# A different first tile, Toeplitz blocks read straight from the taps, and a reordered opening in an attention-and-experts kernel

## The chip, the cores and the metric

The kernel runs on one core of one Trainium2 chip. The metric is the device time of one execution in microseconds (us): the median of three runs, 709.8 us (708.9 to 709.98).

## What is computed

Two layers follow each other. The first is a long convolution that stands in for attention: for each of 32 heads of width 8, all products of the rows of a head of `ctx_2048` (called k; it serves as k and v) are convolved along the 512 positions with the head's filter, a skip term is added, and the result is contracted with the layer-normed `x` (q). The second is a mixture of 16 experts with top-4 routing and a capacity of 256 tokens, plus a shared expert. Everything is float32.

```python
kv = einsum('bhil,bhjl->bijhl', k_, v_)                # k_ = v_ = ctx in heads of 8
y = irfft(rfft(kv, 1024) * rfft(ssm_kernel, 1024))[..., :512]
out = y + kv * D                                       # skip, one number per head
out = einsum('bijhl,bhil->bjhl', out, q_)              # q_ = layernorm(x) in heads
x = x + out
...
h = layernorm(x)
scores = softmax(h @ gate_w.T); top 4 of 16 experts, capacity 256
x = x + sum over chosen experts(silu(h Wg) * (h Wu)) Wd * weight
      + (silu(h sWg) * (h sWu)) sWd                    # shared expert, 704 wide
```

## The kernel before, in words

The 2048 rows (8 batches by 256) are cut into 16 tiles of 128 rows. A tile holds 16 rows of every batch, which is two heads of the convolution (`HT` = 2). The causal convolution is done on TensorE as products with 128x128 Toeplitz blocks: the tile `toep` of a head holds four blocks side by side (offsets 0, 128, 256, 384). A head is done in two halves (`attend`, line 390, called with `c0` = 0 and `c0` = 2, two output chunks of 128 positions each): the first half takes 3 matmuls (1 + 2), the second 7 (3 + 4), all 128x288 (`convolve`, line 404). The trace has two records for each such float32 matmul. From head `PLAIN` = 6 on (tile 3 on) the second half uses five prepared blocks, of which one product, `shared`, serves both chunks: 6 matmuls, a copy of `shared` on ScalarE (line 422) and an extra addition on VectorE (line 427).

The Toeplitz blocks come out of DRAM by overlapping reads, one position further per partition. For the first six heads `blocks` (line 358) reads them from `pad_d`, a copy of the filters with 128 zeros ahead of each and the skip number added to the first tap (lines 257 to 263: two loads on ScalarE's queue, an addition on VectorE at line 262, and the store, on ScalarE's queue again). For the others it reads `win_d`, which `windows` (line 264) writes from `pad` and from two differences, `less` (line 269, GpSimd). A head's `toep` has one of 4 buffers, and `y` in PSUM one of 2.

The steps of a tile, by engine:
- SP's queue loads `kn` (k) and `xs` (x) of a tile (`load_tile`, line 308: k first, then x), 256 KB each.
- TensorE transposes k and normalised q (line 126, four 128x128 transposes each); ScalarE copies the result into `k2`/`q2` (lines 354, 355) and normalises (lines 305, 306). The first two tiles take mean and variance on VectorE (`first_statistics`, line 290: 296, 297, 298) and the root on GpSimd (299, 300); later ones on ScalarE (280 to 285) and GpSimd (286, 287). Tiles from 3 on get k and q into heads by way of DRAM (`send_blocks`, `fetch_blocks`: `sent`, `got`).
- GpSimd forms the products `kv` (`products`, line 374): one of 128x128 (line 379), then four of 128x256 (line 381), chunk by chunk, and from `PLAIN` on a sum of two chunks (line 387).
- VectorE multiplies `y` with q and adds (lines 437, 442, 448, 453, 454). Two smaller sums follow (456, 457): on VectorE for heads below `PLAIN`, on GpSimd for the others.
- `add_to_x` transposes the tile's output back (line 465) and adds it to x (line 467); `new_statistics`, `normalise` and line 646 make the normed, transposed `xnT` of the tile for the second layer; `by_feature` (line 485) computes router logits (line 489) and picks the top experts.

The order is written out by hand: each engine runs its instructions in the order in which the program gives them. The loop over tiles (line 575) does `attend` of tile n and prepares tile n+1 and finishes tile n-1 in between. The shared expert's work (`shared_block`, line 129) is cut into pieces by `yield`; `fill(count)` slips pieces between the halves from the time a tile is ready (`ready`, line 566), so TensorE has work from tile 2 on. Its weights (`swg`, `swu`, `swt`, `swd`) are loaded in 17 pieces by `load_shared(9)`, nine per tile, on SP's queue (line 529). The first product of the first block (line 141, `sgt`) needs both halves of `swt`, which are pieces 9 and 10: the second half is the first piece of tile 1's share. Then come the experts, one after the other (lines 901 on).

All loads named stand in SP's one queue in program order; a wait there holds what is behind it.

Of the kernel before, what the change touches and what calls it, by code (L numbers as in the profile page):

```python
# [20 lines left out]
P = 128  # L21
# [3 lines left out]
NC = L // P  # L25
# [11 lines left out]

ND = HD // 2
PAIRS = ND * HB + HB // 2
PLAIN = 3 * 2  # L40
KW = HB + 3 * B
QW = HB + 4 * B
BACK = 2 * B
# [9 lines left out]
def ssm_attention__then__moe_kernel(  # L53
# [64 lines left out]
    def by_tile(rows):  # L118

        return rows.rearrange("(b n r) l -> n r b l", b=B, n=NT)  # L120
# [126 lines left out]
    with ExitStack() as att:  # L247
# [6 lines left out]

        pad = half.tile([S // HD, P + L], F32, name="pad", tag="k2")
        dcol = const.tile([S // HD, 1], F32, name="dcol")
        nc.vector.memset(pad[:, 0:P], 0.0)
        nc.scalar.dma_start(out=pad[:, P:], in_=ssm)  # L260
        nc.scalar.dma_start(out=dcol, in_=skip)
        nc.vector.tensor_add(pad[:, P : P + 1], pad[:, P : P + 1], dcol)
        nc.scalar.dma_start(out=pad_d[:, :], in_=pad)
        def windows():


# [40 lines left out]

        def load_tile(n):
            kn = load.tile([P, L], F32, name="kn")
            nc.sync.dma_start(out=kn, in_=by_tile(ctx_in)[n])  # L310
            nc.sync.dma_start(out=xs[:, n, :], in_=by_tile(x)[n])
            return kn

        def in_blocks(name):
# [34 lines left out]
        def heads_of(src, width, name):  # L349


            dst = half.tile([P, NC, HT, width], F32, name=name)
            pt = transpose_in(src).rearrange("p c (h w) -> p c h w", h=HT)
            nc.scalar.copy(dst[:, :, :, 0:HB], pt)
            nc.scalar.copy(dst[:, :, :, HB:width], pt[:, :, :, 0 : width - HB])
            return dst
# [33 lines left out]
        def attend(head, hh, c0, toep, kv, q2, oT):  # L390
# [61 lines left out]
            )  # L452
            nc.vector.tensor_mul(yd, yd, view(qq, 0, [[qc, 2], [B, ND], [1, HB]]))  # L453
            nc.vector.tensor_add(f, yd, z[:, :, :, BACK : BACK + HB])  # L454
            adder = nc.vector if head < PLAIN else nc.gpsimd
            adder.tensor_add(f[:, :, 0:2, :], f[:, :, 0:2, :], f[:, :, 2:4, :])  # L456
            adder.tensor_add(
                oT[:, c0 : c0 + 2, hh * HB : (hh + 1) * HB], f[:, :, 0, :], f[:, :, 1, :]
# [23 lines left out]
        def store(n, xn):  # L482
            nc.sync.dma_start(out=by_tile(xw_d[0:T, 0:L])[n], in_=xn)

        def by_feature(n):

            lg = ps_tr.tile([P, E], F32, name="lg", tag="pt")
            for c in range(NC):
                nc.tensor.matmul(  # L489
                    lg, lhsT=xnT[:, c, n, :], rhs=gwT[:, c, :], start=(c == 0), stop=(c == NC - 1)  # L490
                )
            nc.vector.tensor_copy(logits[:, n, :], lg)

            top = tops[:, n, :]
            nc.vector.max(out=top, in_=logits[:, n, :])
            nc.vector.memset(tops[:, n, K:8], 3.0e38)
            rest = small.tile([P, E], F32, name="rest")
            nc.vector.match_replace(
                out=rest, in_to_replace=top, in_values=logits[:, n, :], imm_value=-3.0e38
            )  # L500
            nc.vector.tensor_tensor(sel[:, n, :], rest, logits[:, n, :], ALU.is_lt)

            if n == 0:
                nc.vector.memset(early[:, 0, :], 0.0)
            nc.gpsimd.tensor_add(early[:, n + 1, :], early[:, n, :], sel[:, n, :])

        toeps = {}

        def load_blocks(head):
            toeps[head] = blocks(head)  # L510
# [17 lines left out]
                dst, src = shared_pieces.pop(0)  # L528
                nc.sync.dma_start(out=dst, in_=src)

        loaded = {0: load_tile(0)}
        gw = load.tile([E, L], F32, name="gw", tag="kn")
        nc.sync.dma_start(out=gw, in_=gate_w)
        loaded[1] = load_tile(1)
        load_blocks(0)
        load_blocks(1)

        qn = load.tile([P, L], F32, name="qn", tag="kn")
        k2 = heads_of(loaded.pop(0), KW, "k2")
        stats = first_statistics(xs[:, 0, :])  # L540
        kvs = [products(0, 0, k2)]
        normalise(qn, xs[:, 0, :], *stats)
        kvs.append(products(1, 1, k2))
        q2 = heads_of(qn, QW, "q2")
        pg = ps_tr.tile([P, NC, P], F32, name="pg", tag="pt")
        for c in range(NC):
            nc.tensor.transpose(pg[:, c, 0:E], gw[:, c * P : (c + 1) * P], ident[:E, :E])
        nc.scalar.copy(gwT, pg[:, :, 0:E])

        blocks_left = [(t, 1) for t in range(4)] + [(t, 2) for t in range(4, NT, 2)]
        behind = []

        def fill(count):
# [9 lines left out]

        def ready(n):

            by_feature(n)
            if n + 1 == sum(blocks_left[0]):
                behind.append(shared_block(*blocks_left.pop(0)))  # L570

        making = masks()
        oT_done = None
        sent_k = sent_q = sent_x = got_x = None
        for n in range(NT):
            more = n + 1 < NT
            swift = n + 1 in SWIFT
            oT = work.tile([P, NC, P], F32, name="oT")
            tps = [toeps.pop(n * HT + hh) for hh in range(HT)]
            if more:  # L580
                for hh in range(HT):
                    load_blocks((n + 1) * HT + hh)
            for t in range(2 if n == 0 else n + 3, min(n + 4, NT)):
                loaded[t] = load_tile(t)
            if swift and more:
                got_k, got_q = fetch_blocks(sent_k), fetch_blocks(sent_q)
            load_shared(9)
            if n == 1:
                windows()
            if n:  # L590
                attend(n * HT + 0, 0, 0, tps[0], kvs[0], q2, oT)
            if n - 2 in MILD:
                transpose_blocks(xnT[:, :, n - 2, :], got_x)
            if more:
                if not swift:
                    qn = load.tile([P, L], F32, name="qn", tag="kn")
                    stats = (
                        statistics(qn, xs[:, n + 1, :]) if n else first_statistics(xs[:, 1, :])
                    )
            if n == 0:  # L600
                attend(n * HT + 0, 0, 0, tps[0], kvs[0], q2, oT)
            fill(2)
            if n + 2 in SWIFT:
                kp, kp_by_block = in_blocks("kp")
                kp_stats = statistics(kp_by_block, chunked(xs[:, n + 2, :]))

            attend(n * HT + 0, 0, 2, tps[0], kvs[0], q2, oT)
            if more and not swift:
                k_next = heads_of(loaded.pop(n + 1), KW, "k2")
                normalise(qn, xs[:, n + 1, :], *stats)  # L610
            if n > 0:
                total = add_to_x(n - 1, oT_done)
            fill(2)
            if n > 0:
                xn, xstats = new_statistics(n - 1, total)
            if more:
                if swift:
                    k_next = heads_from(got_k, KW, "k2")
                kv_next = [products((n + 1) * HT, 0, k_next)]

            attend(n * HT + 1, 1, 0, tps[1], kvs[1], q2, oT)
            if more and not swift:
                q_next = heads_of(qn, QW, "q2")
            fill(2)
            if n > 0:
                normalise(xn, xs[:, n - 1, :], *xstats)
                store(n - 1, xn)
                if n - 1 in MILD:
                    xp, by_block = in_blocks("xp")
                    normalise(by_block, chunked(xs[:, n - 1, :]), *xstats)  # L630
                    sent_x = send_blocks(xp)
            if more:
                if swift:
                    q_next = heads_from(got_q, QW, "q2")
                kv_next.append(products((n + 1) * HT + 1, 1, k_next))
            if n + 2 in SWIFT:
                nc.scalar.copy(kp_by_block, chunked(loaded.pop(n + 2)))
                sent_k = send_blocks(kp)
            if n - 2 in MILD:
                ready(n - 2)  # L640

            attend(n * HT + 1, 1, 2, tps[1], kvs[1], q2, oT)
            if n - 1 in MILD:
                got_x = fetch_blocks(sent_x)
            elif n > 0:
                nc.scalar.copy(xnT[:, :, n - 1, :], transpose_in(xn))
                fill(1)
                ready(n - 1)
            fill(1)
            if n + 2 in SWIFT:  # L650
                qp, by_block = in_blocks("qp")
                normalise(by_block, chunked(xs[:, n + 2, :]), *kp_stats)
                sent_q = send_blocks(qp)
            if n in (6, 7, 8):
                next(making)
            oT_done = oT
            if more:
                kvs, q2 = kv_next, q_next
# [5 lines left out]
        nc.scalar.copy(xnT[:, :, NT - 1, :], transpose_in(xn))  # L664
        fill(1)
        by_feature(NT - 1)
        store(NT - 1, xn)
        behind.extend(shared_block(*b) for b in blocks_left)
        fill(1)
# [296 lines left out]
```

## Time and profile before

| what | value |
|---|---|
| time, median of 3 runs | 709.8 us |
| the profiled execution's own time | 708.86 us |
| its span, first to last instruction | 707.1 us |
| TensorE (PE) busy | 679.8 us, 96% |
| VectorE (DVE) busy | 371.4 us, 53% |
| GpSimd (POOL) busy | 294.1 us, 42% |
| ScalarE (ACT) busy | 195.3 us, 28% |
| mean granted TensorE clock | 0.988 |

So 1.8 us of the execution's time lie outside the span, and its time is 0.9 us below the median. A row of the timeline gives the start in us from the span's start, the duration of the stretch, the engine (SPq and ACTq are queues that issue transfers), the line, the operation, what is written <- what is read, and how many records; in brackets stands the idle time before it and what ended it. A row of the windows gives, for a stretch, its length, then busy time and number of records of each engine, the granted TensorE clock, the share of time that the DMA engines were busy, and GB/s. A chain row is one step of the path that ended last.

### The profile page before, as it was taken

The numbers are of one execution on the slowest core, as the hardware profiler recorded it, in microseconds if no ns is written. First come the engines' busy times: TensorE is split into PE (matmuls) and PEld (weight loads), VectorE is DVE, ScalarE is ACT, GpSimd is POOL, SyncE is SP. The second block draws the span as 40 slices with busy tenths as digits, with TensorE's granted clock in tenths as the row PEclk, the third lists the DMA queues.
The fourth block names the chain that finished last, engine by engine and source line by source line (L and its number), as shares of the span: only waits on it lengthen the run. The fifth ranks groups of instructions, "written<-read, shape, count | busy, mean of one in ns | idle before, by whom it ended". The sixth has DMA issues, their size and how long they took to land.

```text
span 707.1 us, 9801 instructions
## 1 busy us (share of the span) xinstructions
PE 679.8 (96%) x3419; PEld 512.1 (72%) x3419; DVE 371.4 (53%) x858; ACT 195.3 (28%) x498; POOL 294.1 (42%) x455
## 2 busy tenths in 40 slices
PE   5899999899999999999999999999999999999994
PEld 3677977777877876876867685777777777777772
DVE  2977666768877676766536411333343334433221
ACT  2443333443432443322222011221222111121120
POOL 5544446767656776556210200233223333322221
PEclk9999999999999999999999999999999999999998
DMA  7942454746566456451019211577777677777732
GB/s 201 308 121 53 128 156 110 184 129 162 148 156 182 115 123 170 127 142 44 16 31 315 58 46 31 168 186 200 217 200 210 186 197 195 209 194 202 190 45 30
DMA packets 89616, 104.03 MB, mean 147 GB/s; under 512 B 10256, under 2 KB 61808, under 8 KB 89568
## 3 DMA queue, kind: packets, MB, share of 16 engines
q1 hardware_dynamic: 82256, 86.22, 43.0%
q0 software_dynamic: 7168, 17.04, 11.7%
q8 instruction: 27, 0.44, 0.3%
q10 hardware_dynamic: 144, 0.15, 0.1%
q14 instruction: 21, 0.17, 0.1%
HBM read 75.73 MB, written 27.66 MB: 146 GB/s over the span
## 4 chain that ended last, share of the span: by engine, by line
PE 90%; DVE 4%; DMA 3%; issue 1%; ACT 1%; SPq 0%; POOLq 0%; POOL 0%; ACTq 0%; DVEq 0%
PE sgu L155 20%; PE y L404 16%; PE pgu L842 15%; PE eo L884 12%; PE so L172 11%; PE pgu L862 4%; PE pt L126 2%; PE pgu L854 2%; PE shared L404 2%; PE sgt L141 2%; PE lg L489 2%; PE ip L747 1%; DMA got<-sent 1%; DVE y L453 1%; PE pt L465 1%; DVE f L454 1%
## 5 line engine op out<-in xcount | busy, mean ns | idle before, releaser
L404 PE MATMUL y<-kv,toep 128*128 128x288 f32 x536 | 145.8, 418 | 3.6 <-POOL rstd L286 2.1
L404 PEld LDWEIGHTS y<-kv,toep 128*128 128x128 f32 x536 | 104.1, 197 | 36.6 <-issue 5.0
L842 PE MATMUL pgu<-xgT,w 128*128 128x256 f32 (+1 forms) x544 | 113.8, 367 | 0.8 <-ACT xgT L814 0.8
L842 PEld LDWEIGHTS pgu<-xgT,w 128*128 128x128 f32 x544 | 98.6, 190 | 20.4 <-issue 7.7
L893 POOL DMA_INDIRECT out<-eo_sb,idx x32 | 51.0, 1595 | 105.6 <-DMA out<-eo_sb,idx 49.3
L801 POOL DMA_INDIRECT g<-xw_d,idx x32 | 32.0, 999 | 141.7 <-PE eo L884 62.4
L381 POOL TENSOR_TENSOR kv<-k 128x256 f32<-128x256 f32 x128 | 86.6, 707 | 0.0
L884 PE MATMUL eo<-wd,mid 128*128 128x512 f32 (+1 forms) x192 | 86.4, 598 | 0.0
L155 PE MATMUL sgu<-xnT,swg 128*128 128x256 f32 (+1 forms) x400 | 78.1, 338 | 1.8 <-DVE tail L149 1.8
L155 PE MATMUL sgu<-xnT,swu 128*128 128x256 f32 (+1 forms) x400 | 78.5, 340 | 0.0
L456 POOL TENSOR_TENSOR f<-f 128x256 f32<-128x256 f32 x52 | 37.9, 728 | 94.6 <-DVE f L454 89.5
L172 PE MATMUL so<-swd,smid 128*128 128x512 f32 x160 | 74.4, 594 | 0.0
L155 PEld LDWEIGHTS sgu<-xnT,swg 128*128 128x128 f32 x400 | 65.4, 191 | 9.2 <-DVE tail L149 2.0
L155 PEld LDWEIGHTS sgu<-xnT,swu 128*128 128x128 f32 x400 | 65.2, 193 | 6.3
L884 PEld LDWEIGHTS eo<-wd,mid 128*128 128x128 f32 (+1 forms) x192 | 35.1, 190 | 37.9 <-issue 33.6
L849 ACT ACTIVATE eact<-pgu 128x256 f32<-128x256 f32 (+1 forms) x34 | 12.6, 371 | 152.1 <-PE pgu L842 152.1
L164 ACT ACTIVATE act<-sgu 128x256 f32<-128x256 f32 (+1 forms) x50 | 17.0, 341 | 129.3 <-PE sgu L155 127.8
L172 PEld LDWEIGHTS so<-swd,smid 128*128 128x128 f32 x160 | 29.7, 190 | 31.0 <-issue 29.2
L850 DVE TENSOR_TENSOR mid<-eact,pgu 128x256 f32<-128x256 f32 (+1 forms) x34 | 13.8, 406 | 70.8 <-ACT eact L849 70.8
L892 DVE TENSOR_SCALAR eo_sb<-eo,g 128x512 f32<-128x512 f32 x32 | 24.0, 751 | 46.3 <-PE eo L884 46.3
L454 DVE TENSOR_TENSOR f<-y,z 128x512 f32<-128x512 f32 x64 | 44.3, 692 | 5.7
L427 DVE TENSOR_TENSOR y<-y,again 128x576 f32<-128x576 f32 x26 | 19.9, 766 | 51.4 <-PE y L404 48.6
(157 smaller groups left out, 852.4 us busy)
## 6 DMA issues: line engine op xcount, KB each, us to landing
w<-in_L_ffn_w_gate SPq DMA_DIRECT2D x16, 704.0 KB, 4.5
w<-in_L_ffn_w_up SPq DMA_DIRECT2D x16, 704.0 KB
got<-sent SPq DMA_DIRECT2D x36, 256.0 KB, 6.0
toep<-win_d SPq DMA_DIRECT2D x26, 320.0 KB, 5.1
wd<-in_L_ffn_w_down SPq DMA_DIRECT2D x16, 512.0 KB, 4.6
kn<-in_ctx SPq DMA_DIRECT2D x16, 256.0 KB, 6.0
xs<-in_x SPq DMA_DIRECT2D x16, 256.0 KB, 6.7
xw_d<-xn SPq DMA_DIRECT2D x16, 256.0 KB, 2.9
```

What stands on the lines that cost most here:

```text
L155: nc.tensor.matmul(pgu[:, k, :], lhsT=sw[:, c, f * P : (f + 1) * P], rhs=toks[:, c, :], start=(c == 0), stop=(c == NC - 1),)
L172: nc.tensor.matmul(po, lhsT=m[:, i * P : (i + 1) * P], rhs=swd[:, (f - 1) % (NF + 1), :], start=(f == 0), stop=(f == NF),)
L381: nc.gpsimd.tensor_mul(kv[:, c, 0 : ND * HB].rearrange("p (d w) -> p d w", d=ND), kh[:, c, 0:HB].unsqueeze(1).broadcast_to([P, ND, HB]), v ...
L404: nc.tensor.matmul(out, lhsT=toep[:, m * P : (m + 1) * P], rhs=rhs, start=(n == 0), stop=(n == len(pairs) - 1),)
L454: nc.vector.tensor_add(f, yd, z[:, :, :, BACK : BACK + HB])
L456: adder.tensor_add(f[:, :, 0:2, :], f[:, :, 0:2, :], f[:, :, 2:4, :])
L801: nc.gpsimd.indirect_dma_start(out=g, out_offset=None, in_=xw_d[:, :], in_offset=bass.IndirectOffsetOnAxis(ap=idx[:, e, n : n + 1], axis=0),)
L842: nc.tensor.matmul(pgu[:, k, cols], lhsT=w[:, k, c, f * P : (f + 1) * P], rhs=xgT[:, c, cols], start=(c == 0), stop=(c == NC - 1),)
L862: nc.tensor.matmul(pgu[:, 0, cols], lhsT=wt[:, c, 0:P], rhs=xgT[:, c, cols], start=(c == 0), stop=(c == NC - 1),)
L884: nc.tensor.matmul(po, lhsT=mid[:m, f, n * P : (n + 1) * P], rhs=wd[:m, f, :], start=(f == 0), stop=(f == NI - 1),)
L892: nc.vector.tensor_scalar_mul(o, po, g[:, L + e : L + e + 1])
L893: nc.gpsimd.indirect_dma_start(out=out, out_offset=bass.IndirectOffsetOnAxis(ap=idx[:, e, n : n + 1], axis=0), in_=o, in_offset=None, comp ...
```

## The change

1. **Order of tiles.** The loop goes through `seq` = 1, 0, 2, 3, ... instead of 0, 1, 2, ... .
2. **Blocks from the taps.** The two heads of tile 1 get `toep` straight from the filters (`load_first`): an overlapping read that begins 127 taps before the head's own filter, in the row of the head before. `begin` then clears what is not the head's in the first block (GpSimd, 128x128) and adds the skip number on an antidiagonal matrix `exch` (VectorE, 128x128, with `skip_b`, the skip numbers on all partitions). The first head's read is two halves on ScalarE's queue, the second's is one on SP's. `pad_d` is still made, for tile 0 alone.
3. **Loads.** x comes before k in `load_tile`. `pad` and `dcol` move from ScalarE's queue to SP's, behind the two tiles; `pad_d` moves to SP's.
4. **ScalarE.** A one-column activation at the start, before anything else but its two loads.
5. **TensorE.** 14 transposes of the identity at the start and 8 between k's and q's transposes, whose result nobody reads (`stir`).
6. **Sums.** Lines 456 and 457 go to GpSimd for the second head of the first two tiles; `PLAIN` is 4, so tile 2 works as tiles 3 on do: `win_d` blocks, `shared`, sums on GpSimd.
7. **Order.** `windows` moves from tile 1's start to the end of the first loop round; in the first round the second head's products come after the first half; the router weight's transposes move behind the second q's; the running count of `sel` on GpSimd gets a function of its own.

```diff
-PLAIN = 3 * 2
+PLAIN = 2 * 2
+        def load_first(queue, hh, width):
+            toep = work.tile([P, L], F32, name="toep", bufs=4)
+            row = ssm[FIRST * HT + hh - 1 : FIRST * HT + hh, L + 1 - P : L]
+            for lo in range(0, L, width):
+                queue.dma_start(
+                    out=toep[:, lo : lo + width],
+                    in_=bass.AP(tensor=row.tensor, offset=row.offset + lo, ap=[[1, P], [1, width]]),
+                )
+            firsts.append(toep)
+        load_first(nc.scalar, 0, 2 * P)
+        idle = const.tile([P, 1], F32, name="idle")
+        nc.scalar.activation(idle, mhalf, AF.Identity)
+        def begin(hh):
+            toep = firsts[hh]
+            nc.gpsimd.affine_select(
...
+            )
+            nc.vector.scalar_tensor_tensor(
+                toep[:, 0:P], exch, skip_b[:, hh : hh + 1], toep[:, 0:P], ALU.mult, ALU.add
+            )
-        nc.scalar.dma_start(out=pad[:, P:], in_=ssm)
-        nc.scalar.dma_start(out=dcol, in_=skip)
-        nc.vector.tensor_add(pad[:, P : P + 1], pad[:, P : P + 1], dcol)
-        nc.scalar.dma_start(out=pad_d[:, :], in_=pad)
+        def load_pad():
+            nc.sync.dma_start(out=pad[:, P:], in_=ssm)
+            nc.sync.dma_start(out=dcol, in_=skip)
+        def pads():
+            nc.vector.tensor_add(pad[:, P : P + 1], pad[:, P : P + 1], dcol)
+            nc.sync.dma_start(out=pad_d[:, :], in_=pad)
...
+            nc.sync.dma_start(out=xs[:, n, :], in_=by_tile(x)[n])
             nc.sync.dma_start(out=kn, in_=by_tile(ctx_in)[n])
-            nc.sync.dma_start(out=xs[:, n, :], in_=by_tile(x)[n])
...
-            adder = nc.vector if head < PLAIN else nc.gpsimd
+            adder = nc.vector if head < PLAIN and hh == 0 else nc.gpsimd
...
+        seq = [FIRST, 0, *range(2, NT)]
+        def stir(count):
+            pt = ps_tr.tile([P, NC, P], F32, name="stir", tag="pt")
+            for i in range(count):
+                nc.tensor.transpose(pt[:, i % NC, :], ident, ident)
+        loaded = {FIRST: load_tile(FIRST)}
+        nc.sync.dma_start(
+            out=skip_b,
+            in_=bass.AP(tensor=skip.tensor, offset=skip.offset + FIRST * HT, ap=[[0, P], [1, HT]]),
+        )
+        load_first(nc.sync, 1, L)
+        stir(14)
         gw = load.tile([E, L], F32, name="gw", tag="kn")
         nc.sync.dma_start(out=gw, in_=gate_w)
+        loaded[0] = load_tile(0)
+        load_pad()
+        qn = load.tile([P, L], F32, name="qn", tag="kn")
+        stats = first_statistics(xs[:, FIRST, :])
+        k2 = heads_of(loaded.pop(FIRST), KW, "k2")
+        normalise(qn, xs[:, FIRST, :], *stats)
+        begin(0)
+        kvs = [products(FIRST * HT, 0, k2)]
+        stir(8)
+        q2 = heads_of(qn, QW, "q2")
+        toeps.update({FIRST * HT + hh: firsts[hh] for hh in range(HT)})
+        stats = first_statistics(xs[:, 0, :])
+        pads()
         load_blocks(0)
         load_blocks(1)
...
-            if more:
+            if more and n:
                 for hh in range(HT):
-                    load_blocks((n + 1) * HT + hh)
+                    load_blocks(seq[n + 1] * HT + hh)
...
-            if n == 1:
-                windows()
+            attend(t * HT + 0, 0, 0, tps[0], kvs[0], q2, oT)
+            if n == 0:
+                begin(1)
+                kvs.append(products(t * HT + 1, 1, k2))
...
+            attend(t * HT + 1, 1, 2, tps[1], kvs[1], q2, oT)
+            if n == 0:
+                windows()
```

## The prediction

> **What bounds the kernel now.** I read the page's busy times first, then the chain that ended last, in order of time, then the stretches of the opening, then its timeline.
>
> ```profile
> PE 679.8 (96%) x3419; PEld 512.1 (72%) x3419; DVE 371.4 (53%) x858; ACT 195.3 (28%) x498; POOL 294.1 (42%) x455
> 1.23 3.57 DMA dcol<-in_L_xattn_D
> 5.07 2.90 DMA pad_d<-pad
> 8.05 3.13 DMA toep<-pad_d
> 11.31 6.68 PE y L404 x20
> ```
>
> TensorE is the bound from some 40 us on, and the change leaves its work there alone (tile 2 apart). What can be won is in the opening. The chain names it: three transfers in a row (skip number, padded filters out, blocks back in), and only at 11.31 the first real matmul.
>
> ```profile
> 11.30:14.50 3.20, 3.19 (x7) 2.35 (x8) 0.00 (x0) 0.00 (x0) 3.12 (x6) 1.00 1.01 257
> 14.50:28.20 13.70, 11.13 (x49) 7.96 (x47) 12.88 (x26) 5.94 (x16) 8.92 (x16) 1.00 0.99 317
> 41.80:45.30 3.50, 3.50 (x12) 2.79 (x11) 2.99 (x11) 1.27 (x3) 2.78 (x5) 0.51 0.24 58
> ```
>
> In the first stretch TensorE makes only 7 records of `y` in 3.2 us, 0.48 apart; from 14.5 they are 0.2425 apart. The records of the clock begin at 14.5, so the 1.00 before that is no measurement: TensorE ran at half rate. In the second stretch VectorE is busy for 12.88 of 13.7 us: it is the bound there, not TensorE. In the third the granted clock is 0.51 again, after TensorE had idled for 0.66 and 0.68 us and done small products.
>
> ```profile
> 4.67 1.09 PE L126 MATMUL pt<-ident,kn 128*128 128x128 f32 x4 [4.67 <-DMA kn<-in_ctx]
> 5.42 1.28 ACT L354 ACT_TABLE_LOAD   x1 [5.42 <-DVE pad L262]
> 14.64 0.29 DVE L437 TENSOR_TENSOR z<-y,q 128x128 f32<-128x128 f32 x1 [5.72 <-PE y L404]
> 25.64 1.44 POOL L269 TENSOR_TENSOR less<-pad 32x256 f32<-32x256 f32 x2
> 26.05 0.59 SPq L529 DMA_DIRECT2D swt<-in_L_ffn_sw_up  x1
> 28.31 3.63 PE L404 MATMUL y<-kv,toep 128*128 128x288 f32 x14 [2.13 <-POOL rstd L286]
> 41.28 1.56 PE L141 MATMUL sgt<-xnT,swt 128*128 128x128 f32 x8
> 46.05 0.97 SPq L369 DMA_DIRECT2D toep<-win_d  x2
> ```
>
> The k copy had its data at 4.67 but waited for ScalarE's table, which stood behind a queue entry waiting for line 262. VectorE gets its first product at 14.64. TensorE's wait at 28.31 is put on GpSimd, but the matmul needs a `y` buffer: VectorE's line 454 released it at 28.17 (27.48 + 0.69).
>
> **The opening, step by step.** Times are from the span's start.
>
> *Loads.* Before, 64 KB (`pad`) and 256 KB (k) had landed at 4.53, x at 5.63, the next tile at 6.83 and 7.80: some 1.1 us per 256 KB. Now x shares the engines with half of the first `toep` (128 KB, ScalarE's queue): 4.9. k stands behind 768 KB in all, 448 more than before: 4.53 + 448 x 1.1/256 = 6.4.
>
> *k's path.* Transposes 0.66 (the warm row; 1.09 cold), copies 0.59 + 0.33: done at 8.0, against 7.52 before. So k's copies come 0.5 us **later**, though the table is ready early (0.8 saved by it, and 1.9 lost by the loads). Products on GpSimd, 0.45 + 4 x 0.67: chunk 1 is there at 9.8, chunk 3 at 11.1.
>
> *q's path.* x at 4.9, statistics 2.0 (5.66 to 7.66 before), ready at 6.9, hidden by k's copies; then 0.29 + 0.81 on ScalarE: 9.1; transposes 0.66: 9.8. `begin(0)` costs 0.29 on GpSimd (the row of the 128x128 select that makes `ident`) and some 0.25 on VectorE; both lie in the wait for k. First `y` at 9.9 instead of 11.31: 1.4 us won.
>
> *Clock.* The first half needs 6 records: 6 x 0.48 = 2.9 us before, 6 x 0.2425 = 1.5 if the clock is up. So 1.4 us hang on whether `stir` turns it up. The nearest row: 1.65 us of transposes from 8.89 to 10.53 did not (the matmuls after them were still 0.48 apart), but they left as much idle. Now there are 3.0 us without a gap (14 x 0.213), then another run from 6.5 to 9.8. [...] I take 1.4 for the sum, with odds of two to one, since no row shows an unbroken run[...]. With it VectorE starts at 11.6 instead of 14.64: 3.0 won.
>
> *VectorE's stretch.* Before: 14.64 to 28.17, 13.5 us for four halves. Now: first half 3.2 + 0.6, because GpSimd makes products beside its sums (line 456 took 0.42 alone and 0.70 beside GpSimd); `begin(1)` 0.25; second half 2.53 + 0.75; third 2.53 and fourth 2.53 without their sums; 0.3 for a `y` that comes last. Sum 12.7: done at 24.4, **3.8 won**. The sums moved to GpSimd (0.73 + 0.46 each) stand in its queue ahead of the next products and of `less`, and wait there for VectorE (21.5 and 24.4).
>
> *To the shared expert.* From that release to `sgt` there were 13.1 us (28.17 to 41.28), through VectorE, line 467, ScalarE, GpSimd's root and two transposes. Nothing of it is removed; I take 13.3: TensorE is ready for `sgt` at 37.7, 3.6 won.
>
> **The new wait.** SP's queue. Before, tile 1's blocks came from `pad_d` and the second half of `swt` was issued at 26.05. Now tile 2's blocks come from `win_d` and stand in SP's queue ahead of it. Products of tile 0's second head end at 25.8, sums 26.9, `less` 28.4 (1.44). `win_d` is stored at 28.4 and lands after 2.3 (the 64 KB `sent` take 1.8, the 80 KB `pad_d` 2.9): 30.7. SP waits there with two `toep<-win_d`, x and k of tile 4, and then `swt`. The same train (2 `toep`, k, x) was issued at 46.05, and x landed 8.5 us later, 7.9 in the next but one (92.63 to 100.55). `swt`'s 128 KB come right behind it: 39.1, between 38.4 and 41. `toep` of tile 2 lands at 34.7 to 36, in time. So `sgt` waits 1.4 us (0.7 to 3.3), and of 3.6 won **2.2 are left**. `swd`, behind it, is needed only some 18 us later (first used at 59.6 before).
>
> **The clock again.** The drop of 41.8 to 45.2 cost half of 3.4 = 1.7 us. The idle time around `sgt` is longer than before, so I expect one drop there too: 0, between +1.7 (none) and -1.7 (two). The other drops (137.4, 168.1) and the waits near them lie in tiles with the same work: 0.
>
> **Tile 2.** In each of its two heads the second half drops from 7 matmuls to 6: 2 x 2 records x 0.2425 = 0.97 us of TensorE's time, on the path. Added: two copies on ScalarE (0.39), two additions on VectorE (0.77), two on GpSimd (0.80), sums on GpSimd (4 x 1.2) instead of VectorE: beside TensorE's work, which is filled with shared-expert pieces; GpSimd was busy for 8.8 of 17 us there. As in tile 3, no stall.
>
> At nothing: `pad`, `dcol` and `pad_d` on SP's queue, behind both tiles (`pad_d` out at some 9.5, landed 2.9 later, the two blocks of tile 0 some 4.5 after that, at 17; needed after TensorE's last half of the first tile, 18.3 + 3.4 = 21.7; without these 4.7 us of cover each us late costs one); x and k of tiles 2 and 3 and the shared pieces behind it on SP start at 13.3 instead of 9.9 and are needed from 28 on; the 8 `stir` after k (1.7 us cold, inside the wait for q from 7.1 to 9.1; uncovered 0.9 at full clock), `exch` (0.5 on idle GpSimd), the router transposes (moved, 0.4), the GpSimd count.
>
> **Sum.** 2.2 + 0.97 = 3.2 us. Profiled execution 708.86 - 3.2 = 705.7; its span 707.1 - 3.2 = 703.9. The median lies 0.9 above the profiled execution: 709.8 - 3.2 = 706.6.
>
> **The rivals.**
> - *The clock isn't turned by `stir`* (20%). For: [...] the row at 8.89. Against: the run is unbroken and twice as long. 1.4 less: 708.0 (707.2 to 708.9).
> - *No wait for `swt`* (20%): the train runs faster than the two I measured, as the queue is empty. Then 3.6 + 0.97 = 4.6: 705.2; and 703.5 if the clock drop at `sgt` goes too.
> - *The gain is used up* (10%): `swt` lands at about 41.5 and a second drop follows the longer idle time: 709.5 (708.9 to 710.3).
> - *Slower* (10%): the same queue, but later. If `win_d` takes the 4.5 us it took before (2.2 more) and the train is held up as at 73.19, where the second `toep` was issued 0.9 later than the first, `swt` comes at 42 to 44, and TensorE, at half clock, starts tile 2 later than before in spite of the earlier start. It decides from 42.3 on (with one more drop) or 44 (without): 711.5.
> - The case of the sum has 40%, 705.6 to 707.7.
>
> **How the numbers follow.** Within 0.2% means 1.4 us, about what a measurement of this kernel can tell from no change. Faster (below 708.4): 40 + 20 + 14 of the 20 of the first rival = 74%. Same: 6 + 10 = 16%. Slower 10%. The range 703.4 to 709.6 leaves out the slower case, half of the used-up one and the tip of the best, under 2 in 10.
>
> **What would show it.** The first `y` at 9.9 and in the chain no `pad_d`; its records 0.24 apart (or 0.48[...]); VectorE's first product at 11.6, its line 454 of the first tile's last half ending at 24.4; ScalarE's table before 3; `less` ending near 28.4; a wait of TensorE at `sgt` on a DMA of `swt`, some 1.4 us; tile 2 without stalls. I am wrong if k lands before 5.5 (then 1 us more is won up to `sgt`), or if GpSimd with its sums makes tile 2's products late (a wait of `y` on line 381 or 387 in tiles 2 and 3).

## The result, and the profile after

The changed kernel takes 705.96 us (median of 19 runs, 702.86 to 708.73), the kernel before, on the same chips, 709.66 us (19 runs, 704.7 to 711.27): a ratio of 0.9951, 95% interval 0.9934 to 0.9967. The forecast said 706.6. The runs of both kernels spread over some 6 us, and why they do turned out to be half of the case. (One execution of the kernel before, beside experiments 1 to 4, fell into a slower state, 799.6 us at a clock of 0.851, and is left out of every mean below.)

The profiled execution of the changed kernel took 702.86 us, with a span of 701.1 and a mean granted clock of 0.995. It is the shortest of its 19 runs, 3.1 us below their median; the profiled one of before was near its own median. So the two profiles differ by 6.0 us in time, where the medians differ by 3.7, and the profiles can't be subtracted blindly.

First the page's busy times, and the head of the chain that ended last, in order of time:

```profile
PE 675.0 (96%) x3437; PEld 510.0 (73%) x3437; DVE 365.1 (52%) x845; ACT 196.1 (28%) x501; POOL 305.8 (44%) x478
13.08 3.42 DMA toep<-pad_d
16.50 1.68 PE y L455 x6
25.16 3.63 PE y L455 x14
33.60 7.12 DMA swt<-in_L_ffn_sw_up
40.76 1.16 PE sgt L141 x8
```

The three transfers no longer stand before the first matmul. In their place one transfer of 7.12 us stands right before `sgt`: the new wait. (The chain's `pad_d` before 16.50 is a wrong lead: that matmul belongs to the second head of tile 1, whose blocks don't come from `pad_d`. What it waited for is `begin(1)`, VectorE's line 299, which ends at 16.23.)

The windows, for the same three stretches: first `y` to VectorE's first product, VectorE's four halves, and the start of the shared expert.

```profile
10.20:11.93 1.73, 1.73 (x10) 1.36 (x9) 0.46 (x3) 0.86 (x2) 1.65 (x5) 1.00 0.10 24
11.93:25.02 13.09, 11.31 (x52) 8.27 (x50) 12.21 (x26) 6.06 (x17) 10.17 (x18) 1.00 0.88 276
40.76:44.17 3.41, 3.41 (x23) 3.10 (x24) 1.04 (x4) 1.27 (x3) 3.41 (x6) 1.00 0.97 271
```

The first stretch is 1.73 us against 3.2; the third runs at full clock, where before it was granted 0.51. The timeline of the opening, what TensorE waited for, and two rows of the kernel before (lines 489 and 155 of its own numbering):

```profile
1.43 3.25 PE L585 MATMUL stir<-ident 128*128 128x128 f32 x14 [1.43 <-POOL mhalf L96]
1.69 1.28 ACT L286 ACT_TABLE_LOAD   x1 [1.69 <-PEq L1026]
7.11 0.66 PE L126 MATMUL pt<-ident,kn 128*128 128x128 f32 x4 [2.44 <-DMA kn<-in_ctx]
10.20 5.02 PE L455 MATMUL y<-kv,toep 128*128 128x288 f32 x20
11.93 0.29 DVE L488 TENSOR_TENSOR z<-y,q 128x128 f32<-128x128 f32 x1 [1.00 <-PE y L455]
24.33 0.69 DVE L505 TENSOR_TENSOR f<-y,z 128x512 f32<-128x512 f32 x1
27.67 1.64 POOL L320 TENSOR_TENSOR less<-pad 32x256 f32<-32x256 f32 x2
32.87 0.63 PE L126 MATMUL pt<-ident,qn 128*128 128x128 f32 x4 [1.74 <-DVE xs L518]
38.01 1.06 PE L540 MATMUL lg<-gwT,xnT 128*128 128x16 f32 x8 [0.68 <-ACT xnT L721]
40.76 1.16 PE L141 MATMUL sgt<-xnT,swt 128*128 128x128 f32 x8 [1.69 <-DMA swt<-in_L_ffn_sw_up]
43.21 1.05 PE L155 MATMUL sgu<-xnT,swg 128*128 128x128 f32 x8
```

```profile
40.36 1.07 PE L489 MATMUL lg<-gwT,xnT 128*128 128x16 f32 x8 [0.68 <-ACT xnT L646]
45.38 1.05 PE L155 MATMUL sgu<-xnT,swg 128*128 128x128 f32 x8
```

Set against before, at marks that both kernels pass:

| mark | before | after | won so far |
|---|---|---|---|
| first `y` | 11.31 | 10.20 | 1.1 |
| VectorE's first product | 14.64 | 11.93 | 2.7 |
| fourth `f` of the first tile done | 28.17 | 25.02 | 3.15 |
| first logits (`lg`) | 40.36 | 38.01 | 2.35 |
| `sgt` | 41.28 | 40.76 | 0.5 |
| first `sgu` | 45.38 | 43.21 | 2.2 |
| second tile's logits | 66.87 | 63.73 | 3.1 |
| fifth logits | 151.58 | 146.94 | 4.6 |
| first expert (`pgu`) | 435.81 | 429.48 | 6.3 |

From there on nothing more is won; at the end of the spans 6.0 are left. The jumps at `sgu` (1.7), the fifth logits (1.5) and the stretch just behind them (1.7) are not work that the change removed: they are the stretches in which the kernel before ran at half clock (41.8, 137.4 and 168.1) and the profiled run of the changed kernel did not. Of the 6.3 us, 4.8 are these three. In this pair structure gave the 0.5 at `sgt` and 1.0 in tile 2. The first rows of the table, though, rest on an opening at full clock that other executions of the same opening did not have: see experiments 1 and 6.

So the theories to be told apart were: (A) the change wins only some 1.5 us by structure, `swt` eats most of the opening's gain, and the rest is the clock, which varies from run to run; (B) the opening's gain is real and the drops are a side issue.

### The profile page after: what moved, and what is told of

It is laid out like the page before. It is cut to its first block, busy times and chain, and to the rows that moved or that the text cites. A ratio compares the mean times of both kernels' runs of the same rounds, so it can differ in the third digit from the quotient of the medians.

```text
span 701.1 us, 9862 instructions
## 1 busy us (share of the span) xinstructions
PE 675.0 (96%) x3437; PEld 510.0 (73%) x3437; DVE 365.1 (52%) x845; ACT 196.1 (28%) x501; POOL 305.8 (44%) x478
## 4 chain that ended last, share of the span: by engine, by line
PE 90%; DMA 5%; DVE 2%; issue 1%; SPq 1%; ACT 0%; POOLq 0%; ACTq 0%; DVEq 0%
PE sgu L155 20%; PE y L455 16%; PE pgu L918 16%; PE eo L960 12%; PE so L172 12%; PE pgu L938 4%; PE pt L126 2%; PE pgu L930 2%; PE shared L455 2%; PE sgt L141 2%; PE lg L540 1%; DMA swt<-in_L_ffn_sw_up 1%; DMA got<-sent 1%; PE ip L823 1%; PE pt L516 1%
## 5 line engine op out<-in xcount | busy, mean ns | idle before, releaser
L455 PE MATMUL y<-kv,toep 128*128 128x288 f32 x528 | 138.6, 407 | 2.7 <-DVE f L505 1.9
L455 PEld LDWEIGHTS y<-kv,toep 128*128 128x128 f32 x528 | 99.1, 190 | 33.1 <-issue 6.3
L507 POOL TENSOR_TENSOR f<-f 128x256 f32<-128x256 f32 x60 | 43.7, 729 | 98.7 <-DVE f L505 93.3
L478 DVE TENSOR_TENSOR y<-y,again 128x576 f32<-128x576 f32 x28 | 21.4, 766 | 53.1 <-PE y L455 50.3
```

The source lines that it names most:

```text
L455: nc.tensor.matmul(out, lhsT=toep[:, m * P : (m + 1) * P], rhs=rhs, start=(n == 0), stop=(n == len(pairs) - 1),)
```

## Experiments

Each ran beside the kernel before; ratios are against it.

**1. `swt` one share earlier**

```diff
-            load_shared(9)
+            load_shared(9 + (n == 0))
```

> The changed kernel, with the second half of swt issued in the first loop round, ahead of the blocks from win_d, in place of behind them. Theory (TensorE waits 1.7 us at sgt for that transfer alone): sgt starts some 0.9 us after the logits' product, at 38.9 in place of 40.76, and everything after it comes 1.8 us earlier: about 704.2 us. Rival (something else is late next, tile 2's blocks or products): the wait moves to the first y of tile 2, the time stays at 706 within 0.5.

Measured: 705.48 us (9 runs), 0.994 (0.9918 to 0.9963). In the profile `sgt` follows the logits by 0.92 us (42.48 to 43.40) instead of 2.75: the wait is gone. But this run's clock fell from 8.7 to 15.5, again at 36.0 and at 165.7, so its marks came late. That the wait goes when `swt` comes earlier is shown; what it is worth in the median isn't, as the intervals overlap.

The profile shows something more. The edit touches nothing before 20 us, so this is the changed kernel's opening a second time, and here `stir` turned the clock up at 5.28 only for it to fall again before the first `y` (10.86):

```profile
1.87:5.28 3.41, 2.81 (x14) 2.40 (x12) 0.00 (x0) 1.31 (x2) 0.68 (x3) 1.00 0.77 180
5.28:8.69 3.41, 1.33 (x12) 1.29 (x12) 1.38 (x4) 0.64 (x2) 1.10 (x3) 1.00 1.08 241
8.69:12.11 3.42, 2.43 (x9) 1.87 (x8) 1.69 (x4) 2.04 (x5) 3.30 (x7) 0.50 0.32 68
14.06 0.29 DVE L488 TENSOR_TENSOR z<-y,q 128x128 f32<-128x128 f32 x1 [2.25 <-PE y L455]
42.48 1.07 PE L540 MATMUL lg<-gwT,xnT 128*128 128x16 f32 x8 [0.68 <-ACT xnT L721]
43.40 1.14 PE L141 MATMUL sgt<-xnT,swt 128*128 128x128 f32 x8
```

VectorE's first product comes at 14.06 instead of 11.93, and the fourth `f` at 27.62 instead of 25.02.

**2. No `stir`**

```diff
-        stir(14)
...
-        stir(8)
```

> The changed kernel without the 22 transposes whose result nobody reads. Theory (they turn the clock up at 5.2): without them the first records of y stand 0.48 us apart for 2 to 3.4 us, VectorE's first product comes 1 to 1.5 us later than 11.93, and the end too: 707 to 707.5 us. Rival ([...] the clock came up at 5.2 for another reason): y at 10.2 with records 0.2425 apart, 706 us.

Measured: 707.28 us (22 runs), 0.9972 (0.9955 to 0.9989). The first `y` records were 0.48 apart, full clock came at 14.1, VectorE's first product at 14.45 instead of 11.93. The medians lie 1.3 us apart, but the two intervals overlap. Runs of equal mean clock can be compared too (it doesn't count the unrecorded opening). At 0.993 the spans are 702.7 and 703.3 with `stir`, 704.2 to 704.7 without; at 0.996 they are 701.6 and 701.8 against 702.7 and 703.3. That is 1.3 to 1.5 us, the forecast's 1.4. At lower clocks the gap is wider: at 0.988 the median span is 704.3 (8 runs) against 707.7 (3). There a recorded half clock of the changed kernel can lie in the opening, as in run 1, where run 2 has it in every run without a record; so 1.4 is what `stir` is worth when it holds.

This run also separates the rest of the change from the clock. Without `stir` the clock's first record comes at 14.1, in the kernel before at 14.5, so their mean clocks count the same stretch. At 0.988 the spans are 707.7 (median of 3) here and 707.7 in the kernel before (median of 48, beside all experiments), at 0.993 they are 704.4 (4) and 703.6 (7): at an equal clock the rest of the change wins nothing. That the median is 2.3 us lower goes with the mean clock, 0.992 over these 22 runs against 0.988.

**3. Tile 1's blocks by way of `pad_d`, as before**, with the rest of the change kept (the padded filters loaded and stored on ScalarE's queue, nothing of `load_first` and `begin`)

```diff
-        load_first(nc.scalar, 0, 2 * P)
+        nc.scalar.dma_start(out=pad[:, P:], in_=ssm)
+        nc.scalar.dma_start(out=dcol, in_=skip)
...
+        nc.scalar.dma_start(out=pad_d[:, :], in_=pad)
...
```

> The changed kernel, but tile 1's blocks come by way of pad_d on the old chain (loads and store on ScalarE's queue, the table ahead of the store); no work on the blocks on GpSimd and VectorE. Theory (the three transfers end at 11.2; the clock and the sums are worth as much as the blocks): first y at 11.3 to 11.5 at full clock, VectorE's first product at 13, but 0.8 to 1.1 us of work on the blocks leaves VectorE's stretch: 706.2 to 707. Rival (the blocks are the gain): near the kernel before, 709.

Measured: 706.38 us (22 runs), 0.9954 (0.9937 to 0.997), no different from the changed kernel. Without the two block reads x landed at 4.33 and k at 5.25 instead of 5.55 and 7.07, so TensorE was ready earlier than in the changed kernel, then waited for `toep<-pad_d` until 11.45:

```profile
11.45 0.82 PE L450 MATMUL y<-kv,toep 128*128 128x288 f32 x1 [2.90 <-DMA toep<-pad_d]
```

The blocks from the taps win 1.25 us at the first `y`; the median doesn't show it.

**4. The sums back on VectorE**

```diff
-            adder = nc.vector if head < PLAIN and hh == 0 else nc.gpsimd
+            adder = nc.vector if head < PLAIN else nc.gpsimd
```

> The changed kernel with lines 456 and 457 of the second heads of the first two tiles on VectorE again. Theory (VectorE bounds the opening up to 35): its stretch grows by 1.1 to 1.4 us per tile in the part before sgt; less and with it swt move only by as much as the last f does, about 0.7 to 1.3: 706.7 to 707.3 us. Rival (the wait at sgt is set by transfers and swallows it): 706 us.

Measured: 705.38 us (22 runs), 0.9956 (0.9935 to 0.9978): the same. (The time outside the span was 2.1 to 2.2 us in these runs, 1.7 to 1.8 in the changed kernel; I don't know why. By spans this kernel is ahead: 703.2 against 704.2.) VectorE's stretch was 13.50 us against 13.09, but `less` ended at 25.98 instead of 29.32, and the queue with it:

```profile
24.53 1.45 POOL L320 TENSOR_TENSOR less<-pad 32x256 f32<-32x256 f32 x2
29.19 0.95 SPq L420 DMA_DIRECT2D toep<-win_d  x2
31.43 0.59 SPq L576 DMA_DIRECT2D swt<-in_L_ffn_sw_up  x1
40.90 1.14 PE L141 MATMUL sgt<-xnT,swt 128*128 128x128 f32 x8
```

`swt` is issued 2.2 us earlier, and `sgt` follows the logits (39.98) without a wait; it starts at 40.90, 0.14 after the changed kernel's. I had expected the sums to be worth 0.7 us or more; what VectorE wins by them, `swt` takes back. (In this run `stir` didn't turn the clock up, so that 0.4 is not the last word: see run 11.)

**5. k ahead of x**

```diff
-            nc.sync.dma_start(out=xs[:, n, :], in_=by_tile(x)[n])
             nc.sync.dma_start(out=kn, in_=by_tile(ctx_in)[n])
+            nc.sync.dma_start(out=xs[:, n, :], in_=by_tile(x)[n])
```

> The changed kernel with k ahead of x in load_tile again. Theory: k then lands at 5.6 and x at 7.1; k's path is 1.5 us earlier, but q's (2.0 statistics, 1.1 normalising, 0.7 transposes) now ends at 10.9, and TensorE's order has it before the first y: y at 10.9 in place of 10.2, 0.5 to 0.7 us more, near 706.5. Rival (k is the bound, as it lands last): y earlier by up to 1.5, 704.5.

Measured: 705.13 us (20 runs), 0.9942 (0.9924 to 0.9961). k lands at 5.83 and x at 7.57; now the path through x decides, q's transposes start at 10.74 and the first `y` at 11.23, 1.0 later than in the changed kernel. The median isn't worse. Loading x first wins 1.0 us at the first `y` that no median shows.

**6. No early activation on ScalarE** (`idle` and its activation left out)

> The changed kernel without the one-column activation at ScalarE's start. Theory: the table load stands behind nothing but two load issues once pad_d's store has left ScalarE's queue, so it still runs at about 1.7 and nothing moves. Rival (the activation is what brings the table early): the load at 7.1 to 8.4, k's copies 0.6 to 1.3 us later.

A single execution, so its time says nothing about the edit: 709.96 us, with four drops of the clock. The first, from 8.45 to 15.27, is that of run 1: VectorE's first product at 13.84, the fourth `f` at 27.39. The table still loads at 1.69 (in the kernel before at 5.42, behind line 262), and k's copies wait for TensorE, not for it. What freed ScalarE's table was the move of `pad` off its queue; in this profile the activation adds nothing.

**7. Longer runs of `stir`**

```diff
-        stir(14)
+        stir(30)
...
-        stir(8)
+        stir(14)
```

> The changed kernel with 30 idle transposes at the start and 14 between k's and q's, so that TensorE has no long pause before the first y. Theory [...]: [...] the mean granted clock of the runs rises and the median falls by 0.5 to 1.2 us, to about 705. Rival (the run of 14 is enough, or transposes count for nothing): 706 within 0.5.

Measured: 704.72 us (6 runs), 0.9928 (0.9904 to 0.9952). Full clock from 5.7 on, the first `y` at 10.32. `swt` landed earlier here (`sgt` at 39.41, a wait of 0.2; I don't know why), but a drop from 39.8 to 43.2 took its place.

**8. `stir` alone, in the kernel before** (14 transposes at the start, 14 between k's and q's)

> The kernel before, with 14 idle transposes at its start and 14 between k's and q's, nothing else. Theory (the half-rate first matmuls were worth 1.4 us, and VectorE bounds what follows): y at 11.3 with records 0.2425 apart, VectorE's first product at 13.1 in place of 14.64, the end 1 to 1.5 us earlier, near 708.3. Rival (transposes don't count): no change, 709.6.

Measured: 709.06 us (22 runs), 0.9997 (0.9981 to 1.0014): nothing. The mean clock shows why: 0.986 over these 22 runs, against 0.988 in the kernel before. At an equal clock of 0.988 the spans are 705.9 (median of 6) against 707.7, so the earlier start is worth some 1.8 us, and about one drop more takes it back. The profile, by luck the fastest of the 22 (704.01 us), shows how. VectorE began 1.58 us earlier (13.06) and was 1.65 ahead at the fourth `f` (26.52). The next `y` began 1.64 us earlier too (26.67, before 28.31), after a wait as long as before (2.13 us, before 2.12). But here the whole wait lay in one stretch of 3.41 us (the kernel before, in steps of 3.41 us from its first record at 14.5, had a border at 28.15, inside the wait), and behind that stretch the clock fell. Its windows:

```profile
23.82:27.23 3.41, 1.28 (x6) 0.70 (x5) 3.27 (x9) 0.00 (x0) 3.07 (x7) 1.00 1.07 293
27.23:30.64 3.41, 3.41 (x9) 2.41 (x8) 3.06 (x8) 0.00 (x0) 0.16 (x1) 0.50 1.08 285
```

TensorE was busy for 1.28 of 3.41 us in the first row, and in the second the clock is 0.50: the 14 records of `y` took 5.32 us, before 3.63. Logits came at 40.40, before 40.36. The drop took back what the start had won.

By now the drops had a pattern. In the profiles so far, those ahead of the last 8 us lasted 3.41 us, or twice that (run 1 from 8.69, run 6 from 8.45), and in the 3.41 us ahead of each TensorE was busy for 0.6 us (run 3, drop at 11.43) to 2.5 (run 7, at 39.82). Two stretches of the kernel before, each with its successor:

```profile
38.40:41.82 3.42, 2.11 (x17) 1.88 (x18) 3.32 (x7) 2.96 (x4) 3.42 (x6) 1.00 0.42 110
41.82:45.23 3.41, 3.41 (x12) 2.69 (x11) 2.97 (x11) 1.27 (x3) 2.76 (x5) 0.50 0.22 54
134.00:137.40 3.40, 1.55 (x14) 1.36 (x13) 3.17 (x9) 0.28 (x1) 3.40 (x7) 1.00 0.68 179
137.40:140.80 3.40, 3.40 (x13) 2.83 (x12) 2.10 (x5) 1.90 (x7) 2.28 (x4) 0.50 0.73 174
```

1.55 of 3.40 is 0.46, by the rounded edges. 2.11 of 3.42 is more, but about half of that are the 16-column products of the logits (1.07 us from 40.36); without them it is about 0.35 (that they may be left out was not shown). The last four runs put this to the test: fill the idle time with transposes that nobody reads.

**9. `swt` early and the long `stir` together** (edits 1 and 7)

> The changed kernel with two edits at once: the second half of swt one share earlier in SP's queue, and longer runs of stir (30 and 14). Theory (the wait at sgt is real, but the stretch after it decides less than the clock): sgt follows the logits by 1.0 us, as in the run with swt early alone, first y stays at 10.2 to 10.4 with records 0.24 apart, and the path to sgu is 1.5 to 1.8 us shorter than in the changed kernel; the median comes to 703.3 to 704.5, under both single edits (705.5 and 704.7). Rival (the idle time that is taken out at sgt only moves a drop of the clock elsewhere, so that the two don't add): 704.7 or more.

Measured: 703.03 us (6 runs, 700.95 to 704.74), 0.9902 (0.9879 to 0.9924). The gains don't cancel each other, though the interval still overlaps that of run 7. In the profile no drop is left between the opening and the last 8 us, in which TensorE has nothing to do, and `sgt` is at 39.27.

**10. The same, with idle transposes in TensorE's waits**

```diff
+        IDLE = {0: 8, 1: 14, 12: 14, 15: 12}
...
+            if c0 == 0:
+                for _ in range(IDLE.get(head, 0)):
+                    nc.tensor.transpose(y[:, 0, 384:512], ident, ident)
...
+            for _ in range(5 if n == 0 else 0):
+                nc.tensor.transpose(lg4[:, 1, :], ident, ident)
```

> The kernel with swt early and the long stir, plus transposes of the identity into unused columns where TensorE waits for VectorE: 8 and 14 in tile 0 (second one of the order), 5 ahead of the first logits, 14 in tile 6 and 12 in tile 7. Theory [...]: the drops near 36, 137 and 168 us are gone, the records show half clock only in the first 6 us, the mean clock is 0.995 or more in nearly every run, and the median is 1.5 to 3 us under that of the kernel without these transposes, with less spread. Rival (the transposes don't count, or the drops have another cause): the same drops at the same places, the median within 0.7 us of it, or above it by the up to 1 us that the transposes delay what is behind them.

Measured: 701.84 us (5 runs, 701.16 to 703.42), 0.9886 (0.9862 to 0.9909). The profile has no half clock between the opening and the last 8 us, and the mean clock of the five runs is 0.995 to 0.997 (0.990 to 0.996 in run 9). The transposes fill the waits:

```profile
31.21 1.69 PE L487 MATMUL y<-ident 128*128 128x128 f32 x14
33.12 0.63 PE L126 MATMUL pt<-ident,qn 128*128 128x128 f32 x4 [0.22 <-DVE xs L523]
128.33 1.69 PE L487 MATMUL y<-ident 128*128 128x128 f32 x14
132.13 1.16 PE L155 MATMUL sgu<-xnT,swg 128*128 128x128 f32 x8 [0.32 <-DVE tail L149]
62.12 0.71 PE L546 MATMUL lg<-ident 128*128 128x128 f32 x5
```

The waits of 1.74 and 1.84 us are down to 0.22 and 0.32. The five ahead of logits went to tile 0, the second one of the order, where TensorE does not wait (last row): they cost 0.55. The median is 1.2 us under run 9's (the intervals overlap), less than the 1.5 that I expected at least, since run 9 kept the clock up in several of its runs already; the 0.55 are in it.

**11. Run 10 with the sums back on VectorE** (edit 4)

> As the kernel with the idle transposes, but the two sums of the second heads are back on VectorE. With the clock held up, the sums' own worth shows. Theory (measured 0.4 us in VectorE's stretch, and GpSimd's less and the products beside it late by as much): the fourth f ends 0.4 us later, less ends 1 to 3 us earlier, and the median is within 0.5 us of the kernel with the sums shared. Rival (the forecast's term, 0.75 us for the sharing): 0.7 to 1 us slower.

Measured: 702.3 us (5 runs, 701.92 to 702.46), 0.9887 (0.9865 to 0.9909). With the clock up before the first `y` VectorE's stretch is 14.15 us (12.28 to 26.43) against 13.09 in run 10, so the sums are worth 1.06 there, more than in run 4; the logits come 0.76 later and the first expert 0.43 (428.86 against 428.43), but the spans end alike: 699.9 against 700.0 in the profiles, 700.1 in the median of both. The 0.46 between the medians lies outside the span, 2.2 us here and 1.7 in run 10, as in run 4. `less` ends 4.9 us earlier (24.67 against 29.57), more than the 3 expected; nobody needs it then, since `swt` no longer stands behind it. My correction after run 4 was too strong: sharing the sums is worth 1 us where it is made, nothing that shows in the span at the end, and in the changed kernel, with `swt` behind `win_d`, nothing either.

**12. The kernel before with idle transposes** (run 8, and 18 in tile 1, 5 ahead of the first logits, 14 in tile 6, 12 in tile 7)

> The kernel before, with stir (14 and 14) and idle transposes in the same waits: 18 in tile 1, 5 ahead of the first logits, 14 in tile 6 and 12 in tile 7. With the clock held up in both, what is left between this kernel and the changed one with the same transposes is structure. Theory (of the profiled pair's 6.3 us some 4.8 were drops of the clock, and the earlier clock is worth 1.4): this kernel comes to 703.5 to 706, 4 to 6 us faster than before, and the changed kernel with swt early and the transposes is 2.5 to 4 us under it. Rival (the drops explain little): 708 to 709.5, as with stir alone.

Measured: 703.93 us (6 runs, 702.94 to 705.19), 0.9914 (0.9893 to 0.9936). Seventy-seven transposes whose results nobody reads, without one line of the change, win more than the change does (3.7 us by the medians): 6.4 us. Run 10 is 2.1 us below it, a bit under the 2.5 expected. That is not yet structure at an equal clock: the mean clock is 0.992 here and 0.995 in run 10, about one drop more (the profile has one from 12.4 to 15.9, in the opening). So 2.1 us is about the most that the change's structure, with `swt` early, can be worth.

## Why the prediction was right, and where it was wrong

The number and the direction held: 3.7 us faster where 3.2 were forecast. The way there held in part only, and two errors cancelled.

- **Loads.** x at 4.9 was 5.55, k at 6.4 was 7.07. I had summed bytes; run 3 shows the price of sharing: without the two overlapping block reads k landed 1.8 us earlier. As the waits overlap (q's copies ran behind k's, as forecast), the first `y` was only 0.3 late: 10.20.
- **Clock by `stir`.** The mechanism and its size were right where it holds: 1.4 us, by run 2. How often it holds was not. Six profiles have these 22 transposes: in five the clock was up by 5.3 us, in run 4 only at 12.44; but in runs 1 and 6 it fell again before the first `y`, in runs 3 and 5 at 11.4 and 11.8. Only the changed kernel's own profile kept it through the opening, and that was luck. The forecast saw that `stir` could fail, not that the clock could fall again behind it: in run 1 it did after a stretch (5.28 to 8.69) in which TensorE was busy for 1.33 us and waited for k the rest of the time. The changed kernel's own profile has such a stretch too (5.20 to 8.61, busy for 1.50; the wait for k ends at 7.11 after 2.44 us), and there the clock stayed up. The longer runs of transposes kept it up through the opening in all four profiles (7, 9, 10 and 11). Transposes alone came ahead of full clock in run 7: TensorE did nothing else from 2.27 to 5.69, busy for all of the 3.42 us. The trace records them as plain matmuls.
- **VectorE's stretch.** 12.7 was 13.1, done at 25.0 instead of 24.4, so 3.15 of the 3.8 were won. The sums' term was too large (0.75 for each of two halves, 1.06 for both in run 11); `begin(1)` was too small, 0.78 beside GpSimd where 0.25 stood.
- **From there to `sgt`.** "Nothing of it is removed; I take 13.3": TensorE was ready 13.9 us after the release (at 38.93, if `sgt` follows the logits by 0.92 as it did before). A wait that I did not see: q's transposes at 32.87 wait 1.74 us for line 518 on VectorE, where before they waited for ScalarE and TensorE alone. The line frees one of the two `pt` buffers; the router's transposes, which use the same buffers, had moved. Behind them stand the last half of tile 0 and the transposes of `xn`, at 36.73, though `xn` was ready at 35.90: 0.8 us, by the trace. No run tried it.
- **The `swt` wait.** The mechanism and its size were right: 1.69 us, forecast 1.4 (`less` ended 0.9 late, `swt` landed at 40.7, in the range). But at `sgt` only 0.5 was won and not 2.2, since TensorE itself was 1.2 late and `swt` 1.6. This is the mis-sized term.
- **The clock after that.** "I expect one drop there too: 0", "the other drops: 0". This is the step that failed. The three of the kernel before cost 1.5 to 1.7 us each, and whether one falls varies from run to run: near 36, 138 and 169 us runs 5 and 6 have one each, run 4 and the changed kernel's profile none. The stretches of 3.41 us don't lie alike either (the first record of the clock comes at 4.6 to 7.1 in the profiles in which early transposes turned it up); that how they lie over the waits decides is my reading, and no run shows it. The mean clock was 0.990 over the 19 runs of the changed kernel, and 0.988 over those of the kernel before beside the experiments. One drop is 0.0024 (half of 3.41 us over a span of 707), so by this count the change has 0.7 of a drop less, some 1.3 us. The count is not quite like for like, since the clock's first record comes at 5.2 in the changed kernel's profile and at 14.5 in that of the kernel before: at the same 0.988 the changed kernel's median span is 704.3 (8 runs), that of the kernel before 707.7 (48). In run 2, where the count is like for like, 1.5 drops less make up the whole gain. So fewer drops made good at least a part of what `sgt` lacked; how much of the 3.7 us they are is open.
- **Tile 2.** `sgu` to the logits takes 20.52 us against 21.49: 0.97, as worked out, and no stall. Runs 1 and 4, without idle transposes in that stretch, show the same 20.52, and run 8, with the old tile 2, 21.49.

So theory A fits better than B, with one correction: the 0.5 + 1.0 us of structure up to the second logits include 1.4 from the earlier clock, and so need an opening at full clock. Two things remain open: how the 3.7 us of the medians divide between structure and clock, and why there are fewer drops. The change keeps TensorE busier in some waits and leaves others longer (33 and 40 us), and a mean over 19 runs doesn't say which.

## What to carry to other kernels

Before costing a change of under 1% on TensorE, compare the mean granted clock of several runs: here 0.0024 is one drop, 1.8 us by the line through 115 runs of the kernel before, and a single profile can hold three more of them than the next. See first what that mean counts: not the opening before the first record (up to 14.5 in the kernel before), but the last 6 to 8 us, which are at half clock in every profile with TensorE done (in the changed kernel's from 694.7, its last matmul ended at 691.4), and cost no time. A gain ahead of a wait can be lost to a drop behind it (run 8: 1.64 us won, 1.69 lost), so close the idle stretches first. Transposes that nobody reads, at the start and in waits that exist anyway, were worth 6.4 us to the kernel before. And when an engine's work is moved to another, look for the queue behind the instruction that it delays: the sums cost nothing on GpSimd itself, and a wait of 1.7 us by way of `less`, `win_d` and SP's queue.

## What the runs showed of the hardware

- **When the clock turns.** Stretches are counted in steps of 3.41 us from the records of the clock. Full clock came after stretches with TensorE busy for 2.81 us (run 1, from 1.87), 3.18 (run 4, from 9.03) and 3.42 (run 7, from 2.27, transposes alone). After 2.48 (run 4, from 2.20, first row below) and 2.43 (run 1, from 8.69) it did not. It fell after stretches with 0.57 (run 3, from 8.02) to 1.57 us (run 6, from 134.74), and after some with more in which products of 16 columns are counted: 1.76 (run 12, from 9.02) and 2.03 to 2.52 (most in run 7, from 36.4). But stretches with 1.45 and 1.50 were also survived, in the kernel before from 24.74 and in the changed kernel from 5.20. In run 6 two stretches have nearly the same, 1.56 and 1.57, from 127.91 and from 134.74, and the clock fell only after the second. So the busy time of one stretch, as the profile has it, doesn't decide alone. Run 4, which failed, and run 7, which did not (the clock's column reads 1.00 until its first record):

```profile
2.20:5.61 3.41, 2.48 (x12) 2.07 (x10) 0.00 (x0) 0.97 (x2) 0.41 (x2) 1.00 0.86 202
2.27:5.69 3.42, 3.42 (x18) 3.42 (x17) 0.05 (x1) 0.91 (x2) 0.34 (x2) 1.00 0.96 201
```

- **Drops without one long gap.** The drop at 137.4 in the kernel before followed waits of 1.84 us and less; the longest idle time of TensorE between 20 and 200 us in any profile here is 2.6 us (run 5, up to 132.06), less than one stretch.
- **Two engines at once.** The 128x256 addition on VectorE took 0.42 us with GpSimd idle (the kernel before, line 456 at 17.11) and up to 1.00 with GpSimd busy (run 11, at 19.07).
